# A graph attention layer and a dot-product attention layer on one core: x1 made in the head buffer in groups of four row tiles beside two held row tiles of layer 1; x1 transposes in pairs; finer pieces and VectorE sums in entry 0

## Chip, core and metric

The kernel runs on one core of a Trainium2 chip, in float32. The core has a matrix engine (TensorE, PE in the profile, with PEld for its weight loads), a vector engine (VectorE, DVE), a scalar engine (ScalarE, ACT), GpSimd (POOL) and SyncE (SP), which here only issues DMA transfers. Each engine works through its own queue in order; engines wait for one another with semaphores. The metric is the device time of one execution in microseconds. Times below come from three runs and from one further execution that the hardware profiler recorded.

## What is computed

There are B = 8 entries of N = 2048 nodes and D = 256 channels, one 0/1 adjacency matrix for all, and two layers. Layer 0 has H = 8 heads of 32 channels with an additive score; layer 1 has one head with a dot-product score. Each layer adds its input and normalizes the rows. The reference, cut to that:

```python
def layer0(x, adj, W, a_src, a_dst, beta_tilde, W_out):
    x_proj = einsum('bnd,hdf->bhnf', x, W)
    e = leaky_relu(e_src[..., :, None] + e_dst[..., None, :], 0.2)   # e_src, e_dst: x_proj times a_src, a_dst
    e = e + (softplus(beta_tilde) * log(adj + 1e-6))
    attn = softmax(where(adj > 0, e, -max), axis=-1)
    h = einsum('bhij,bhjf->bhif', attn, x_proj)
    return h.transpose(0, 2, 1, 3).reshape(B, N, D) @ W_out.T

def layer1(x, adj, W1, W2, W3):
    e = leaky_relu(einsum('bnd,bmd->bnm', x @ W1, x @ W2), 0.2)
    attention = softmax(where(adj > 0, e, -1e12), axis=-1)
    return relu(einsum('bnm,bmd->bnd', attention, x @ W3))

x = layernorm(x + layer0(x, adj, ...))       # called x1 below
x = layernorm(x + layer1(x, adj, ...))       # the output
```

## The kernel before

*Tiles.* Nodes go in NT = 16 row tiles of P = 128; channels in KC = 2 halves of 128; heads in NP = 4 pairs. PSUM has three tiles of 128 x 512 for passing results (`mm_tile`, tag "mm"), and one place each for `val`, `den` (128 x 1024) and `acc`. SBUF pools hold buffers by tag: "s" has four, "c" three, "mt", "d" and "p" two each, "pen" one, "ht" (in the pool `chunk`) three, "row" four. A buffer comes free when its last reader is done.

*Layer 0.* `Gat.project` (L225) loads x, transposes it, and multiplies it by the weights and by the score vectors; from that come v (values times exp of the destination score), re (two factors per node and head) and the rows c (a function of the source score), which for entries 1 to 7 are stored in DRAM and loaded back by `load` (L283) and `query_rows` (L289). The softmax is written so that an unnormalized weight is s = max(c, re) * mt, where mt is a row tile of the transposed adjacency raised to beta. One *unit* is one head pair and one row tile jt (`Gat.step`, L295): two DVE instructions make s for the two heads (L311, 128 x 2048 each); PE multiplies them by v into `val`, and by exp of the destination score into `den`, the denominators (both through `products`, L336). For row tiles in a list per entry, `SUMMED` (L67), the second product is left out; instead DVE keeps running sums d of s times that factor (L318; the first is a copy on ACT, L324), and at jt = 15 a product with ones adds the two sums to `den` (L329). Entry 0 has an empty list. With the last unit of a head pair, `finish` (L340) copies val and den out of PSUM on ACT, sends the denominators through DRAM to get their reciprocals in the right shape (four transfers, a reciprocal, a store, and after every second pair four loads into `rb`), and multiplies the heads by them (L363). An entry has 64 units.

*Between the layers.* `output` (L365) loads x into the buffer "h3"; for each of the 16 row tiles it multiplies the heads by W_out (y, L376), adds x (L378), normalizes (`layer_norm`, L199, with four ACT instructions on one column each, L206 to L209, and the scaling, L210) and stores x1 to DRAM through SP (L380). `turn` (L383) transposes x1, a row tile at a time, into the buffer "x1t" and multiplies it by W3 (L396), overwriting "h3".

*Layer 1.* `Dot` (L402): `queries` (L411) multiplies x1 by W1 W2^T for 512 rows; `scores` (L420) makes a row tile's scores, prelu on the way out of PSUM (L428), mask and row maximum on DVE (L431), exp on ACT (L432). One *step* (L435) is one row tile: it transposes the exponentials (L445), makes the next row tile's scores (L426), and multiplies by h3 into `acc` (L461); then it scales, adds x1 (loaded again, L466), normalizes, and stores the row tile of the output through SP (L471). A step takes a function `fill`, called at its start, after the scores and at its end (k = 0, 1, 2), which puts other work there.

*Order.* PE's instructions run in the order of the program text (`manual_schedule`, L86). A scheduler orders the other engines. So the loop at the end sets the order:

```python
    for k in range(NP * NT):
        gats[0].step()
        ...
    for b in range(1, B + 1):
        ...
        if dot is not None:
            dot.step()
        layer_0(2)
        for k, _ in enumerate(gat.output()):
            if k % 8 == 7:
                layer_0(1)
        for k, _ in enumerate(gat.turn()):
            if k % 2 == 1:
                layer_0(1)
        dot = Dot(gat)
        dot.step(lambda k: layer_0((2, 1, 1)[k]))
        for i in range(NT - 2):
            dot.step(lambda k: layer_0((0, 2 - (i % 2 == 1), 2 - (i % 14 == 13))[k]))
    dot.step()
```

Here `layer_0(n)` runs n units of entry b, and the first `dot.step()` is row tile 15 of entry b - 2. Entry 0 runs its 64 units alone, in the first head pair together with `make_mt` (L163), which makes the 16 tiles mt from the adjacency (ACT Ln and Exp, DVE, PE transposes, four ACT copies) and stores them, and throughout with 42 pieces of the other entries' projections (six an entry: four of 512 rows each, the scaling of v, the rows c) and from the second pair on with pieces of `later_weights`. After that, 12 units of entry b stand in the boundary between entry b - 1's layers, and 52 in its layer 1 steps. The last boundary and the last layer 1 have no units beside them.

Of the kernel before, what the change touches and what calls it, by code (L numbers as in the profile page):

```python
# [18 lines left out]
P = 128  # L19
# [8 lines left out]
def kernel(  # L28
# [38 lines left out]
    SUMMED = [(), (1, 3, 6, 9, 12)] + [(1, 3, 6, 8, 11, 13)] * (B - 2)  # L67
# [39 lines left out]
    def load_x(b, half):  # L107
        xr = wide.tile([P, NT // 2, D], F32, tag="p", name="xr", bufs=2)
        nc.sync.dma_start(xr, x[b].rearrange("(t p) d -> p t d", p=P)[:, ts(half, NT // 2), :])
        return xr  # L110

    first_x = [load_x(0, half) for half in range(2)]


# [18 lines left out]
    def later_weights():  # L133
# [3 lines left out]
        for w, dst in ((w_out, wot), (w1, w1t), (w2, w2t)):  # L137
            src = wide.tile([P, KC, D], F32, tag="pen", name="square", bufs=1)
            nc.sync.dma_start(src, w.rearrange("(k p) c -> p k c", p=P))
            yield  # L140
            for kc in range(KC):
                t = mm_tile("sq_t")
                for o in range(KC):
                    nc.tensor.transpose(t[:, ts(o, P)], src[:, o, ts(kc, P)], ident)
                nc.scalar.copy(dst[:, kc, :], t[:, 0:D])
# [17 lines left out]
    def make_mt(jt):  # L163
# [7 lines left out]
        nc.vector.scalar_tensor_tensor(m, a, 0.0, m, ALU.is_gt, ALU.mult)  # L171
        mt = wide_tile("mt", "mt", 2)
# [43 lines left out]
    class Gat:  # L216


        def __init__(self, b):
            self.b = b  # L220
            self.units = ((hp, jt) for hp in range(NP) for jt in range(NT))
            self.hts = []
            self.mts = []

        def project(self):  # L225
# [6 lines left out]
            xrs, xts = [], []  # L232

            def turn(g):
                if g % 2 == 0:
                    xrs.append(load_x(b, g // 2) if b > 0 else first_x[g // 2])
                xt = chunk.tile([P, KC, BK], F32, tag="ht", name="xt", bufs=3)
                for kc in range(KC):
                    t = mm_tile("tr")
                    for k in range(IG):  # L240
                        nc.tensor.transpose(t[:, ts(k, P)], xrs[-1][:, g % 2 * IG + k, ts(kc, P)], ident)
                    nc.scalar.copy(xt[:, kc, :], t)
                xts.append(xt)

            turn(0)
            for g in range(NB):
                if g + 1 < NB:
                    turn(g + 1)
                for k in range(IG):
                    it = g * IG + k  # L250
                    t = mm_tile("proj")
                    for kc in range(KC):
                        nc.tensor.matmul(t[:, 0:D + 2 * H], xts[g][:, kc, ts(k, P)], wp[:, kc, :],
                                         start=(kc == 0), stop=(kc == KC - 1))
                    nc.scalar.copy(v[:, it, :], t[:, 0:D])
                    nc.scalar.copy(both[:, it, :], t[:, D:D + 2 * H])
# [38 lines left out]
        def step(self, count=1):  # L295

            for _ in range(count):
# [6 lines left out]
                while first and len(self.mts) < min(jt + 2, NT):  # L304
                    self.mts.append(make_mt(len(self.mts)))
# [9 lines left out]
                chain = SUMMED[self.b]  # L315
# [5 lines left out]
                if jt in chain[:1]:  # L321
                    self.sums = [wide_tile("d", "d", 2) for _ in heads]
# [17 lines left out]
        def finish(self, hp):  # L340
# [3 lines left out]
            if lo == 0:  # L344
                self.hts.append(whole.tile([P, N], F32, name=f"ht{hp // 2}"))
            ht = self.hts[-1]
            for s in range(2):
                nc.scalar.copy(ht[lo:lo + HP * DH, ts(s, HALF)], self.val[ts(s, HP * DH), :])
# [14 lines left out]
            nc.vector.tensor_mul(ht, ht, rb)  # L363

        def output(self):  # L365
# [3 lines left out]
            self.h3 = h3 = whole.tile([P, NT, D], F32, tag="h3", name="h3")  # L369
            xb = x[b].rearrange("(t p) d -> p t d", p=P)  # L370
            for g in range(NB):
                nc.sync.dma_start(h3[:, ts(g, IG), :], xb[:, ts(g, IG), :])
            for it in range(NT):
                y = mm_tile("y")
                for g, ht in enumerate(self.hts):
                    nc.tensor.matmul(y[:, 0:D], ht[:, ts(it, P)], wot[:, g, :], start=(g == 0), stop=(g == 1))  # L376
                z = h3[:, it, :]
# [167 lines left out]
```

## Time and profile before

| | us |
| --- | --- |
| median of three runs | 4469.75 (4466.98 to 4470.57) |
| the profiled execution | 4467.18 |
| its span | 4465.4 |
| end of entry 0's last unit | 538.7 |
| first L416 product of entries 0 to 7 | 633.3, 1151.4, 1664.2, 2176.5, 2687.1, 3200.0, 3712.4, 4189.2 |
| from the last of these to the end | 276.2 |
| idle time of DVE before its waits for an mt transfer | 19.9 |
| wait of SP's queue for z before the stores of the output (L471) | 698.3 |

Three kinds of stretch follow one another. Entry 0's layer 0 fills the first 538.7 us. Then come, for each entry, a boundary (from the last unit of the entry's layer 0 to the first L416 product) and a layer-1 stretch; a period of the two is 510.6 to 518.1 us between the first L416 products of entries 0 to 6. The last period is shorter by the missing units, and after it comes the last layer 1.

In the rows of the profile, a name such as `s<-c,re,mt` gives output and inputs of an instruction by the program's names; L311 is line 311 of the kernel above. Where a wait is given in square brackets, it is the idle time of that engine ahead of the row and the instruction that ended it. A page's busy shares are means over all stages, so a stage has to be read by a window of its own.

### The profile page before, as it was taken

How to read it: one execution, taken by the hardware profiler on the slowest of the kernel's cores; microseconds unless marked ns; L12 is line 12 of the kernel's file. 1: busy time of each engine (PE TensorE's matmuls, PEld its weight loads, DVE VectorE, ACT ScalarE, POOL GpSimd, SP SyncE). 2: the span in 40 equal slices, each digit the busy share in tenths (PEclk: the TensorE clock that was granted, in tenths of full speed). 3: DMA queues.
4: the chain of work that ended last, by engine and by line, in shares of the span. 5: the costliest groups of instructions: out<-in, count | busy, mean ns of one | idle time of the engine just before them, and what ended most of it. 6: DMA issues, size and time to landing. Idle time of an engine off the chain costs nothing.

```text
span 4465.4 us, 60558 instructions
## 1 busy us (share of the span) xinstructions
PE 4267.6 (96%) x24988; PEld 2217.3 (50%) x24988; DVE 3631.8 (81%) x2605; ACT 1758.7 (39%) x3611; POOL 7.5 (0%) x14
## 2 busy tenths in 40 slices
PE   6899899999999999999999999999999999999899
PEld 4444344445455545555455544545454554554566
DVE  5778798888989988988899888888988888898222
ACT  5622233334333343334333343333433343333555
POOL 0000000000000000000000000000000000000000
PEclk8999999999999999999999999999999999999999
DMA  7777665666555555556555565555545565553211
GB/s 217 262 264 263 249 218 204 220 233 217 180 189 193 182 193 184 188 181 224 176 182 178 186 213 187 189 181 207 194 160 190 189 216 183 187 182 134 69 50 41
DMA packets 252773, 843.62 MB, mean 189 GB/s; under 512 B 33616, under 2 KB 152400, under 8 KB 176976
## 3 DMA queue, kind: packets, MB, share of 16 engines
q1 hardware_dynamic: 252496, 839.74, 54.0%
q8 instruction: 196, 3.21, 0.3%
q14 instruction: 81, 0.66, 0.0%
HBM read 763.76 MB, written 75.37 MB: 188 GB/s over the span
## 4 chain that ended last, share of the span: by engine, by line
PE 60%; DVE 14%; issue 8%; ACT 4%; DMA 1%; SPq 0%; DVEq 0%; ACTq 0%
PE acc L461 17%; PE e L426 15%; PE val L336 12%; DVE s L311 9%; PE den L336 8%; PE pt L445 4%; DVE d L318 3%; PE h1p L416 2%; ACT p L432 1%; PE h3p L396 1%; ACT h L210 1%; DVE p L431 1%; PE y L376 1%; DMA mt<-mt_d 0%; ACT f L206 0%
## 5 line engine op out<-in xcount | busy, mean ns | idle before, releaser
L311 DVE SCALAR_TENSOR_TENSOR s<-c,re,mt 128x2048 f32<-128x2048 f32 x1024 | 2350.6, 2343 | 209.6 <-PE den L336 159.9
L336 PE MATMUL val<-s,v 128*32 128x512 f32 x8192 | 1045.3, 607 | 78.7 <-DVE s L311 78.5
L461 PE MATMUL acc<-h,pts 128*128 128x256 f32 x4096 | 950.6, 380 | 14.9 <-ACT pts L447 14.4
L426 PE MATMUL e<-x1t,h 128*128 128x512 f32 x2048 | 904.0, 594 | 0.0
L461 PEld LDWEIGHTS acc<-h,pts 128*128 128x128 f32 x4096 | 748.2, 190 | 107.7 <-ACT pts L447 21.8
L336 PE MATMUL den<-s,re 128*32 128x512 f32 x5568 | 709.2, 598 | 0.0
L318 DVE SCALAR_TENSOR_TENSOR d<-s,re,d 128x2048 f32<-128x2048 f32 x272 | 632.4, 2343 | 0.0
L426 PEld LDWEIGHTS e<-x1t,h 128*128 128x128 f32 x2048 | 379.6, 190 | 450.1 <-issue 417.9
L336 PEld LDWEIGHTS val<-s,v 128*32 128x32 f32 x8192 | 240.9, 110 | 697.8 <-issue 526.3
L447 ACT COPY pts<-pt 128x512 f32<-128x512 f32 x512 | 296.1, 583 | 664.7 <-PE pt L445 664.4
L428 ACT ACTIVATE p<-e 128x512 f32<-128x512 f32 x512 | 302.5, 595 | 432.3 <-PE e L426 432.3
L431 DVE CUSTOM_DVE_ANT_0 p<-p,pen 128x2048 f32<-128x2048 f32 x128 | 292.7, 2287 | 205.9 <-ACT p L428 205.6
L336 PEld LDWEIGHTS den<-s,re 128*32 128x32 f32 x5568 | 194.2, 112 | 426.7 <-issue 426.6
L432 ACT ACTIVATE p<-p,neg 128x2048 f32<-128x2048 f32 x128 | 256.7, 2005 | 272.5 <-DVE neg L431 272.5
L445 PEld LDWEIGHTS pt<-ident,p 128*128 128x128 f32 x2048 | 238.0, 141 | 223.5 <-issue 167.2
L445 PE MATMUL pt<-ident,p 128*128 128x128 f32 x2048 | 318.7, 279 | 5.4 <-ACT p L432 5.4
L469 DVE TENSOR_TENSOR z<-z,x1r 128x256 f32<-128x256 f32 x128 | 54.0, 422 | 205.4 <-ACT z L468 197.0
L468 ACT ACTIVATE z<-acc,rec 128x256 f32<-128x256 f32 x128 | 60.6, 473 | 355.9 <-PE acc L461 330.3
L376 PE MATMUL y<-wot,ht 128*128 128x256 f32 x512 | 129.6, 414 | 37.4 <-DVE ht L363 36.3
L206 ACT ACTIVATE f<-mv,eps_ln 128x1 f32<-128x1 f32 x256 | 74.2, 290 | 199.0 <-DVE mv L204 198.1
L396 PE MATMUL h3p<-w3s,x1t 128*128 128x256 f32 x512 | 133.4, 386 | 12.3 <-ACT x1t L392 12.3
L376 PEld LDWEIGHTS y<-wot,ht 128*128 128x128 f32 x512 | 104.7, 208 | 68.3 <-DVE ht L363 39.2
(76 smaller groups left out, 2083.6 us busy)
## 6 DMA issues: line engine op xcount, KB each, us to landing
mt<-mt_d SPq DMA_DIRECT2D x496, 1024.0 KB, 4.8
c<-c_d SPq DMA_DIRECT2D x64, 1024.0 KB, 6.7
pen<-pen_d SPq DMA_DIRECT2D x112, 512.0 KB, 3.3
xr<-in_x_dram SPq DMA_DIRECT2D x16, 1024.0 KB, 7.1
adj_t<-in_adj_dram SPq DMA_DIRECT2D x16, 1024.0 KB, 6.8
mt_d<-mt SPq DMA_DIRECT2D x16, 1024.0 KB, 5.6
rb<-rec_d SPq DMA_DIRECT2D x64, 256.0 KB, 4.0
h<-in_x_dram SPq DMA_DIRECT2D x32, 512.0 KB, 5.9
```

Source lines behind the costliest of these rows:

```text
L311: nc.vector.scalar_tensor_tensor(sa, self.cs[a], self.re[:, 0, jt, h:h + 1], mt, ALU.max, ALU.mult)
L318: nc.vector.scalar_tensor_tensor(d, sa, e[:, jt - 1, h:h + 1], d, ALU.mult, ALU.add)
L336: nc.tensor.matmul(dst[ts(q, DH), ts(c, BK)], weights[q % 2], s[q % 2][:, ds(q // 2 * HALF + c * BK, BK)], start=start, stop=stop)
L376: nc.tensor.matmul(y[:, 0:D], ht[:, ts(it, P)], wot[:, g, :], start=(g == 0), stop=(g == 1))
L396: nc.tensor.matmul(t[:, 0:D], x1t[:, kc, ts(it - 1, P)], w3s[:, kc, :], start=(kc == 0), stop=(kc == KC - 1))
L426: nc.tensor.matmul(t, self.h1[:, kc, ts(it % IG, P)], self.x1t[:, kc, ts(c, BK)], start=(kc == 0), stop=(kc == KC - 1))
L428: nc.scalar.activation(p[:, ts(c, BK)], t, AF.Prelu, alpha=ALPHA)
L431: nc.vector.tensor_tensor_reduce(p, p, pen, -1.0, FMAX, ALU.add, ALU.min, neg)
L432: nc.scalar.activation(p, p, AF.Exp, bias=neg, scale=-1.0, accum_out=den)
L445: nc.tensor.transpose(t[:, ts(k, P)], p[:, ts(g * IG + k, P)], ident)
L447: nc.scalar.copy(pt, t)
L461: nc.tensor.matmul(acc, now[:, ts(k, P)], self.h3[:, j, :], start=(j == 0), stop=(j == NT - 1))
```

## The change

The diff has five parts.

1. *Entry 0.* `SUMMED[0]` gets six row tiles, used by head pairs 1 to 3 (in the first, `first`, the list is empty); the running sums lie in the buffers "p". Projection pieces are one row tile of 128 each (18 an entry, 126 in all), and are done four units before entry 0's end. x for them is loaded in groups of four row tiles through the buffer "pen", one ahead. `make_mt` is split: `make_m` runs one row tile earlier. The square weights are loaded in halves into "row" buffers.
2. *Head buffer.* The two buffers `ht0` and `ht1` become one, tag "heads", with a row tile's two channel halves side by side. x1 is made in place in it, where it lay in "h3" before.
3. *Output.* `output` works in groups of four row tiles: y in pairs (one 512-wide add for two row tiles), statistics for each row tile, then Ln, Exp and a product for four columns at once (`f4`), four scalings, and one store of x1 for four row tiles. x is loaded in groups of four through the "ht" buffers of `chunk`, three at first and the fourth after the first group.
4. *Turn.* Transposes and W3 products go by two row tiles, with one 512-wide ACT copy each; a unit follows every pair.
5. *Order and queues.* The last two steps of layer 1, row tiles 14 and 15 of the entry before, are held back behind the end of the entry's units; row tile 14 has two units of the next entry beside it, row tile 15 has the four groups of `output` (1, 1 and 2) and two units. The other steps carry 4, 4 and 3 units in turn. Stores of the output and of x1 are issued by ACT instead of SP.

```diff
-    SUMMED = [(), (1, 3, 6, 9, 12)] + [(1, 3, 6, 8, 11, 13)] * (B - 2)
+    SUMMED = [(1, 3, 6, 8, 11, 13), (1, 3, 6, 9, 12)] + [(1, 3, 6, 8, 11, 13)] * (B - 2)
...
         for w, dst in ((w_out, wot), (w1, w1t), (w2, w2t)):
-            src = wide.tile([P, KC, D], F32, tag="pen", name="square", bufs=1)
-            nc.sync.dma_start(src, w.rearrange("(k p) c -> p k c", p=P))
+            src = [row_tile("square") for _ in range(KC)]
+            for o in range(KC):
+                nc.sync.dma_start(src[o], w[ts(o, P), :])
...
+    def x_groups():
+        for b in range(1, B):
+            for g in range(NB):
+                xg = wide.tile([P, IG, D], F32, tag="pen", name="xg", bufs=1)
+                nc.sync.dma_start(xg, x[b].rearrange("(t p) d -> p t d", p=P)[:, ts(g, IG), :])
+                yield xg
...
-    def make_mt(jt):
+    def make_m(jt):
         a = wide.tile([P, NT, P], I32, tag="d", name="adj_t", bufs=2)
...
         nc.vector.scalar_tensor_tensor(m, a, 0.0, m, ALU.is_gt, ALU.mult)
+        return m
+
+    def make_mt(jt, m):
         mt = wide_tile("mt", "mt", 2)
...
             def turn(g):
-                if g % 2 == 0:
-                    xrs.append(load_x(b, g // 2) if b > 0 else first_x[g // 2])
+                if b == 0:
+                    xr = first_x[g // 2][:, ds(g % 2 * IG, IG), :]
+                else:
+                    xr = ahead.pop() if ahead else next(groups)
...
+                if b > 0:
+                    ahead.extend(xg for xg in [next(groups, None)] if xg is not None)
             turn(0)
-            for g in range(NB):
-                if g + 1 < NB:
+            for it in range(NT):
+                g, k = divmod(it, IG)
+                t = mm_tile("proj")
...
+                nc.scalar.copy(v[:, it, :], t[:, 0:D])
+                nc.scalar.copy(both[:, it, :], t[:, D:D + 2 * H])
+                if k == 0 and g + 1 < NB:
                     turn(g + 1)
...
                 yield
...
                 while first and len(self.mts) < min(jt + 2, NT):
-                    self.mts.append(make_mt(len(self.mts)))
+                    at = len(self.mts)
+                    while len(self.ms) < min(at + 1 + (jt > 0), NT):
+                        self.ms.append(make_m(len(self.ms)))
+                    self.mts.append(make_mt(at, self.ms[at]))
...
-                chain = SUMMED[self.b]
+                chain = () if first else SUMMED[self.b]
...
-                    self.sums = [wide_tile("d", "d", 2) for _ in heads]
+                    self.sums = [wide_tile("d", "d" if self.b else "p", 2) for _ in heads]
...
-            if lo == 0:
-                self.hts.append(whole.tile([P, N], F32, name=f"ht{hp // 2}"))
-            ht = self.hts[-1]
+            if hp == 0:
+                self.ht = whole.tile([P, NT, KC, P], F32, tag="heads", name="ht")
+            ht = self.ht[:, :, hp // 2, :]
...
         def output(self):
...
-            for g in range(NB):
-                nc.sync.dma_start(h3[:, ts(g, IG), :], xb[:, ts(g, IG), :])
-            for it in range(NT):
-                y = mm_tile("y")
-                for g, ht in enumerate(self.hts):
-                    nc.tensor.matmul(y[:, 0:D], ht[:, ts(it, P)], wot[:, g, :], start=(g == 0), stop=(g == 1))
-                z = h3[:, it, :]
-                nc.vector.tensor_add(z, y[:, 0:D], z)
-                layer_norm(z)
-                nc.sync.dma_start(x1_d[b, ts(it, P), :], z)
-                yield
+            def load(g):
+                xs.append(chunk.tile([P, IG, D], F32, tag="ht", name="xg", bufs=3))
+                nc.sync.dma_start(xs[g], xb[:, ts(g, IG), :])
+            for g in range(NB - 1):
+                load(g)
+            for g in range(NB):
+                if g == 1:
+                    load(NB - 1)
...
+                z = self.ht[:, ts(g, IG)].rearrange("p t k i -> p t (k i)")
+                for k in range(0, IG, 2):
+                    y = mm_tile("y").rearrange("p (t c) -> p t c", t=2)
+                    for i in range(2):
+                        for kc in range(KC):
+                            nc.tensor.matmul(y[:, i, :], self.ht[:, g * IG + k + i, kc, :], wot[:, kc, :],
+                                             start=(kc == 0), stop=(kc == KC - 1))
+                    nc.vector.tensor_add(z[:, k:k + 2, :], y, xs[g][:, k:k + 2, :])
+                    for i in range(k, k + 2):
+                        nc.vector.bn_stats(st[:, i, :], z[:, i, :])
+                        nc.vector.bn_aggr(mv[:, i, :], st[:, i, :])
+                f = small.tile([P, 2, IG], F32, name="f4", bufs=2)
+                nc.scalar.activation(f[:, 0, :], mv[:, :, 1], AF.Ln, bias=eps_ln)
+                nc.scalar.activation(f[:, 0, :], f[:, 0, :], AF.Exp, scale=-0.5)
+                nc.vector.scalar_tensor_tensor(f[:, 1, :], mv[:, :, 0], -1.0, f[:, 0, :], ALU.mult, ALU.mult)
+                for k in range(IG):
+                    nc.scalar.activation(z[:, k, :], z[:, k, :], AF.Identity, bias=f[:, 1, k:k + 1],
+                                         scale=f[:, 0, k:k + 1])
+                nc.scalar.dma_start(x1_d[b].rearrange("(t p) d -> p t d", p=P)[:, ts(g, IG), :], z)
+                yield
...
         def turn(self):
...
-            for it in range(NT + 1):
-                if it < NT:
+            for j in range(NT // 2 + 1):
+                if j < NT // 2:
                     t = mm_tile("tr1")
                     for kc in range(KC):
-                        nc.tensor.transpose(t[:, ts(kc, P)], h3[:, it, ts(kc, P)], ident)
-                    nc.scalar.copy(x1t[:, :, ts(it, P)], t[:, 0:D].rearrange("p (k i) -> p k i", k=KC))
+                        for i in range(2):
+                            nc.tensor.transpose(t[:, ts(kc * 2 + i, P)], self.ht[:, 2 * j + i, kc, :], ident)
+                    nc.scalar.copy(x1t[:, :, ts(j, 2 * P)], t.rearrange("p (k i) -> p k i", k=KC))
...
-            nc.sync.dma_start(out[self.b, ts(it, P), :], z)
+            nc.scalar.dma_start(out[self.b, ts(it, P), :], z)
...
-    pieces = (B - 1) * (NB + 2)
+    pieces = (B - 1) * (NT + 2)
     for k in range(NP * NT):
         gats[0].step()
-        for _ in range((k + 1) * pieces // (NP * NT) - k * pieces // (NP * NT)):
+        due = [min(i * pieces // (NP * NT - 4), pieces) for i in (k, k + 1)]
+        for _ in range(due[1] - due[0]):
             next(others)
...
-        if dot is not None:
-            dot.step()
-        layer_0(2)
-        for k, _ in enumerate(gat.output()):
-            if k % 8 == 7:
-                layer_0(1)
-        for k, _ in enumerate(gat.turn()):
-            if k % 2 == 1:
-                layer_0(1)
+        rows = gat.output()
...
+        if dot is None:
+            layer_0(2)
+            for _ in range(2):
+                output(2)
+                layer_0(1)
+        else:
+            dot.step(lambda k: layer_0((0, 0, 2)[k]))
+            dot.step(lambda k: (output((1, 1, 2)[k]), layer_0((0, 1, 1)[k])))
+        for _ in gat.turn():
+            layer_0(1)
         dot = Dot(gat)
         dot.step(lambda k: layer_0((2, 1, 1)[k]))
-        for i in range(NT - 2):
-            dot.step(lambda k: layer_0((0, 2 - (i % 2 == 1), 2 - (i % 14 == 13))[k]))
+        for i in range(NT - 3):
+            dot.step(lambda k: layer_0((0, 2 - (i % 3 == 2), 2)[k]))
+    dot.step()
     dot.step()
```

## The prediction

> **What bounds the kernel now.** I read the page's busy shares, then the busy time by stage, then the order of time where TensorE (PE) stood still.
>
> ```profile
> PE 4267.6 (96%) x24988; PEld 2217.3 (50%) x24988; DVE 3631.8 (81%) x2605; ACT 1758.7 (39%) x3611; POOL 7.5 (0%) x14
> ...
> L311 DVE SCALAR_TENSOR_TENSOR s<-c,re,mt 128x2048 f32<-128x2048 f32 x1024 | 2350.6, 2343 | 209.6 <-PE den L336 159.9
> ```
>
> PE leads, VectorE (DVE) follows. The 96% is a modelled busy share and a mean over stages, so the stages decide. Columns of the next view: stretch, its length, busy time (instructions) of PE, PEld, DVE, ACT, POOL, granted clock, DMA share, GB/s.
>
> ```profile
> 54.00:212.00 158.00, 130.39 (x910) 72.08 (x913) 122.09 (x63) 101.00 (x158) 0.36 (x1) 0.92 0.80 258
> 212.00:538.70 326.70, 295.96 (x2068) 131.84 (x2060) 253.74 (x124) 75.03 (x244) 6.03 (x6) 0.96 0.70 255
> 538.70:633.30 94.60, 79.03 (x485) 37.00 (x482) 86.08 (x82) 34.49 (x117) 0.00 (x0) 0.91 0.60 206
> 3104.90:3200.00 95.10, 85.18 (x516) 45.55 (x512) 83.23 (x84) 39.57 (x125) 0.00 (x0) 0.95 0.57 198
> 3200.00:3617.20 417.20, 415.83 (x2432) 209.69 (x2432) 367.99 (x236) 158.34 (x270) 0.00 (x0) 1.00 0.53 187
> 4130.20:4189.20 59.00, 44.60 (x213) 37.62 (x210) 17.96 (x53) 33.14 (x122) 0.00 (x0) 0.88 0.32 97
> ```
>
> The rows are: entry 0's first head pair; its other three; then, from the end of an entry's last layer-0 unit (call it T) to L416 of its layer 1, the first such boundary and one of six steady ones; a layer-1 stretch (15 steps, 52 units); the last boundary. The layer-1 stretch is PE from end to end at clock 1.00. Time can be had in the boundaries and in entry 0. In the boundary PE waits for the head product, and DVE's own queue holds it up:
>
> ```profile
> 3119.85 0.70 PE L376 MATMUL y<-wot,ht 128*128 128x256 f32 x2
> 3125.13 2.50 PE L376 MATMUL y<-wot,ht 128*128 128x256 f32 x5 [4.58 <-DVE ht L363]
> ...
> 3100.19 0.43 DVE L469 TENSOR_TENSOR z<-z,x1r 128x256 f32<-128x256 f32 x1 [4.44 <-ACT z L468]
> 3103.27 4.61 DVE L311 SCALAR_TENSOR_TENSOR s<-c,re,mt 128x2048 f32<-128x2048 f32 x2 [1.97 <-PE den L336]
> ...
> 3154.47 9.13 DVE L311 SCALAR_TENSOR_TENSOR s<-c,re,mt 128x2048 f32<-128x2048 f32 x4
> 3163.52 2.35 DVE L318 SCALAR_TENSOR_TENSOR d<-s,re,d 128x2048 f32<-128x2048 f32 x1
> ```
>
> Four s products take 9.05 us start to start, 2.26 each. From 3154 to 3200 DVE has no gap: it, not PE, ends the boundary.
>
> **Prices.** From the order of time after 3215: a row tile's first transposes 0.49, its scores 6.97 (3216.38 to 3223.35), its weighted sum 8.22 (3227.41 to 3235.63); a step without units is 15.7 us. A unit is 1.74 (val) plus 1.72 (den, unless the sums have it). A pair of s, or of running sums, is 4.52 on DVE.
>
> **Six steady boundaries.** An entry's last unit now stands in step 13, not 14, so one whole step moves behind T. The stretch before T falls by 15.7 to 401.5 us with the same 52 units. DVE's work there stays 368 less one p reduction of 2.3: 91% instead of 88%, in lumps of two sum pairs. I charge 1 us of new waits (bounds 0 and 6).
>
> Behind T I follow the order in which the built kernel queues its instructions, by hand (new lines are marked so). Step 14 takes PE to T+15.7, two units to T+21.0. In the last boundary, where DVE is idle, the head product L363 starts at T+16.7 (4146.9 against 4130.2) and takes 2.3; so the 4.58 us wait is covered. On SP the load of v, nine transfers of the denominators and three x loads stand ahead of unit 2's mt load, which has until T+28; the fourth x load waits for the first adds (T+25) with unit 3's mt load behind it, which at 4.8 us to land is in time for T+36. Then:
> - y of four row tiles ends at T+28.4. DVE takes each two tiles as one add, two statistics, two aggregates: 0.7 + 0.8 + 0.4 = 1.9. The 512-wide add isn't in the trace; between one and two of the 256-wide (0.41, L378) I take 0.7. In DVE's queue one s of unit 2 stands behind the third add and the other behind the fourth: done at T+34.6. PE waits 6.
> - unit 2, the weighted sum, y of the last four pairs of tiles, val of unit 3: PE at T+55.5. The s of units 3 and 4 and one sum pair hold DVE to T+49.2, the last two groups' normalization to T+58. The last aggregate is queued behind an s; ACT has that group's Ln ahead of the first x1t copy, for which new L439 waits: PE stands about 5, to T+61.
> - unit 4 ends at T+66.4 and frees the s buffers of unit 6. Six units and two sum pairs on DVE, 36.2, end at T+102.6; the last val at T+104.4.
>
> So this part grows from 95.1 to 104.4 while 15.7 leaves the stretch before: -6.4, with the new waits -5.4, times six = -32. If all three waits vanish it stays 95.1: -15.7 each. If they grow by half it is 112: +1. I take what the replay gives, since the order is fixed and its durations stand in rows.
>
> A rule speaks against groups of four. The rows: L206 to L209 take 0.29, 0.20, 0.19 and 0.29 us for one column each, on ACT at 39%. The Trainium skill (Perfetto Trace Analysis, Optimizing Scalar/DVE Operations) has grouping pay on a saturated engine, and smaller pieces where an unsaturated one makes others wait. By it the saved columns buy nothing and the wait before T+61 is their price; with finer pieces unit 6 would start 4.2 earlier and the six would give -58.
>
> **Last boundary** (59.0). No s work: y from T+19.2, the weighted sum between, last y at T+42.3; the last group's Ln frees the copies at T+46; eight pairs of 0.43 + 1.74 make T+63.5. With the step moved: -15.7 + 4.5 = -11 (bounds -16 and -3). **First boundary** (94.6). 12 units as before. PE waits 9.93 before its first val, for c rows behind the last est; those now come four units earlier, but v can't be loaded until its last use, 7.9 us (v<-v_d, median): -2 (bounds -6 and +4).
>
> **Entry 0.** First head pair, 158 us: m is made one tile earlier, so Ln and Exp (2.0 each) run under two s products. A unit needs on DVE 2 x 2.26 + 2.20 + 1.13 = 7.9 (83.44 to 85.64, 87.90 to 89.03), on ACT 4.0 + 2.4 for four mt copies + 1.8 for two pieces of projection = 8.2; DMA is already at 0.80. I take 8.9, and 5.4 for one scaling of v (L260 to L270): 148, so -10 (bounds -27, by DVE alone, and 0). Other three pairs, 326.7 us: 15 den products leave PE (-25.8), 30 sums come to DVE (30 x 2.26 = 67.9); six 2.0 us copies go to ACT, busy 23% there. DVE then needs 321.6 and PE 270, the latter spread evenly by pieces of one row tile: DVE is the bound, -5. This is the loosest guess: if only half of the 73 us that DVE idles there now goes, +31; if the 0.08 by which its records overlap comes off each, -15.
>
> **Queues, copies, weights.** Outputs and x1 leave SP for ACT. SP waited 698.3 us on z for the outputs (its waits), but DVE only 19.9 for mt: bounds -20 and 0, and I take 0, as the stretch where outputs run has no PE gap to give. SP issues an output in 0.34; ACT's issue is not shown, 0 to 0.58 (four x loads in 2.31), 20 an entry, covered by PSUM's three score tiles; uncovered it is 8 x 20 x 0.34 = 54. Copies of 512 for two of 256 (583 ns against 372 twice) lie behind DVE: 0. The weights in halves lie under entry 0's DVE: 0.
>
> The page DMA: Bandwidth & Descriptors, Issuing engines are not separate DMA queues, grants a second issuing engine only its issue time: by it 0.34 x 128 = 44 us of SP and nothing on the path. The page PSUM — Partial Sum Buffer, Engine vs sequencer instructions, calls ScalarE's queue strictly first in, first out; no row here shows what a transfer in it costs.
>
> **Sum.** -32 - 11 - 2 - 10 - 5 = -60. The profiled execution took 4467.18 us (span 4465.4); the median of the runs, 4469.75, is 2.6 above. 4467.2 - 60 + 2.6 = 4410.
>
> **Rivals.**
> - *DVE gives it back.* Steady boundaries end at T+109.8, net 0, and entry 0 gains nothing: -11 - 2 = -13, 4457. For it: DVE is busy 88% of the boundary already. Against: DVE idles 4.44 + 1.97 + 2.25 + 4.69 + 1.98 = 15.3 us before its rows from 3100 to 3118, which the moved step fills.
> - *The waits I charge vanish.* 6 x (-15.7 + 1) - 16 - 2 - 10 - 5 = -121, 4349. For it: L311 at 3091.10 shows an entry's first s done long before T. Against: only four s buffers.
> - *ACT's queue becomes the gate (slower).* A moved transfer may have to wait on ACT for an earlier one that holds its completion semaphore; Prelu and copies stand behind, and PE runs only two score tiles ahead (2 x 1.74 = 3.5 us). At mt's 4.8 to land plus 0.34 PE loses 1.6 an output: 128 x 1.6 = +205, 4615. It decides from 3.5 + 60/128 = 4.0 us held. For it: nearly all moved transfers carry such a wait in the new order. Against: the earlier transfer lies about a step (28 us) back.
>
> **Numbers.** Forecast 0.54, first rival 0.18, second 0.16, slower 0.12. The likeliest gives 4410 (alone 4385 to 4435). The range reaches over the first rival and into the second, and leaves out the slower one and the second's far half: 4360 to 4462. 0.2% (9 us) is what a measurement here can tell from no change; of the first rival 0.06 falls within it: faster 0.82, same 0.06, slower 0.12.
>
> **What would show it.** From one entry's first queries product (L416, new L459) to the next, 507 us instead of 512.4; no PE gap before the first y, but 6 before unit 2 and 5 before the first L439; a layer-1 stretch near 402 without PE gaps; DVE near 95% busy from entry 0's second head pair on, and its T near 523 instead of 538.7. I am wrong if ACT waits at DMA rows between Prelus, if entry 0 passes 550, or if a boundary stays under 97.

## The result, and the profile after

The changed kernel takes 4463.76 us (median of four runs, 4461.57 to 4465.11) against 4469.22 beside it: a ratio of 0.9988, 95% interval 0.9971 to 1.0005. That is 5.5 us, and not told from no change; 4410 was forecast. The profiled execution spans 4462.5 us against 4465.4, 2.9 shorter. Cut into the prediction's stages (T is the end of an entry's last layer-0 unit):

| stage, us | before | forecast | after |
| --- | --- | --- | --- |
| T of entry 0 | 538.7 | 523.7 | 559.5 |
| first boundary | 94.6 | 92.6 | 95.3 |
| steady boundary (from 3105) | 95.1 | 104.4 | 105.6 |
| layer-1 stretch behind it | 417.9 | 402.5 | 403.3 |
| period, first L416 (L459) product to the next | 512.4 | 507 | 508.6 |
| last boundary | 59.0 | 63.5 | 63.1 |
| last layer 1 | 276.2 | 276.2 | 276.2 |

The boundary and the stretch that were replayed came out within 1.2 us. (The prediction's row for the stretch before, 417.2, ends 0.7 us ahead of its last product; measured to that product it is 417.9.) Entry 0 did not: 20.8 us longer where 15 shorter were forecast. That is 35.8 of the 57 us between the forecast change (-60) and that of the profiled executions (-2.9). The six steady boundaries have another 17.3, the first boundary 2.7 and the last 1.1. The page's lines for the two engines, and DVE's two large groups:

```profile
PE 4254.7 (95%) x24748; PEld 2217.8 (50%) x24748; DVE 3688.7 (83%) x2603; ACT 1682.0 (38%) x3041; POOL 13.4 (0%) x14
...
L330 DVE SCALAR_TENSOR_TENSOR s<-c,re,mt 128x2048 f32<-128x2048 f32 x1024 | 2354.2, 2342 | 178.8 <-PE den L355 117.7
...
L337 DVE SCALAR_TENSOR_TENSOR d<-s,re,d 128x2048 f32<-128x2048 f32 x302 | 701.7, 2344 | 0.0
```

There are 240 fewer matmuls and 30 more running sums, as the prediction counted them; the sums went from 632.4 to 701.7 us. The busy time by stage, with the columns of the prediction's view:

```profile
56.00:212.00 156.00, 135.10 (x920) 72.28 (x921) 122.83 (x63) 101.65 (x162) 0.36 (x1) 0.89 0.80 253
212.00:559.50 347.50, 293.12 (x1813) 130.19 (x1811) 326.24 (x157) 86.07 (x247) 11.95 (x6) 0.91 0.69 247
559.50:654.80 95.30, 76.75 (x483) 39.91 (x480) 79.78 (x76) 24.24 (x43) 0.00 (x0) 0.89 0.58 194
3105.00:3210.60 105.60, 96.72 (x579) 55.04 (x576) 85.13 (x85) 35.95 (x69) 0.00 (x0) 0.97 0.59 200
3210.60:3613.90 403.30, 401.71 (x2373) 199.38 (x2370) 365.13 (x231) 150.77 (x255) 0.00 (x0) 1.00 0.54 189
4123.20:4186.30 63.10, 58.09 (x274) 46.95 (x274) 20.79 (x55) 31.14 (x66) 0.00 (x0) 0.97 0.33 101
```

The second row is entry 0's head pairs 1 to 3. DVE is busy 326.2 us there, near the 321.6 of the forecast, but in 347.5 us: 94%, not all of it. That is the "near 95% busy" that the prediction gave as a sign; at 95%, 321.6 us of work take 338.5, so that the sign and the -5 did not go together. PE is busy 293.1 us with 1813 matmuls where it took 296.0 for 2068 before; the granted clock is 0.91 against 0.96, so the 15 products that left bought no PE time.

In order of time, the steady boundary shows the waits that the prediction named (PE first, then DVE; h3p is x1 times W3):

```profile
3125.92 3.72 PE L408 MATMUL y<-wot,ht 128*128 128x256 f32 x16
...
3135.05 1.04 PE L355 MATMUL val<-s,v 128*32 128x512 f32 x2 [1.52 <-DVE s L330]
3138.70 2.78 PE L355 MATMUL val<-s,v 128*32 128x512 f32 x11 [2.60 <-DVE s L330]
...
3165.86 1.99 PE L439 MATMUL h3p<-w3s,x1t 128*128 128x256 f32 x8 [2.70 <-ACT x1t L434]
```

```profile
3132.05 0.69 DVE L410 TENSOR_TENSOR ht<-y,xg 128x512 f32<-128x512 f32 x1
3132.66 2.34 DVE L330 SCALAR_TENSOR_TENSOR s<-c,re,mt 128x2048 f32<-128x2048 f32 x1
...
3135.66 0.66 DVE L410 TENSOR_TENSOR ht<-y,xg 128x512 f32<-128x512 f32 x1
...
3136.33 2.32 DVE L330 SCALAR_TENSOR_TENSOR s<-c,re,mt 128x2048 f32<-128x2048 f32 x1
```

PE has no gap before the first y. It waits 1.52 + 2.60 before unit 2 (6 forecast), whose two s stand behind the third and the fourth add, as said, and 2.70 before the first h3p (5 forecast).

### The profile page after: what moved, and what is told of

The parts are those of the page before. It is cut to its first block, busy times and chain, and to the rows that moved or that the text cites. A ratio compares the mean times of both kernels' runs of the same rounds, so it can differ in the third digit from the quotient of the medians.

```text
span 4462.5 us, 59194 instructions
## 1 busy us (share of the span) xinstructions
PE 4254.7 (95%) x24748; PEld 2217.8 (50%) x24748; DVE 3688.7 (83%) x2603; ACT 1682.0 (38%) x3041; POOL 13.4 (0%) x14
## 4 chain that ended last, share of the span: by engine, by line
PE 60%; DVE 14%; issue 7%; DMA 3%; ACT 2%; SPq 0%; ACTq 0%; DVEq 0%
PE acc L504 16%; PE e L469 15%; PE val L355 12%; DVE s L330 9%; PE den L355 8%; PE pt L488 4%; DVE d L337 4%; DMA mt<-mt_d 2%; PE y L408 2%; PE h1p L459 2%; PE h3p L439 1%; DVE p L474 0%; ACT p L475 0%; DMA rc<-dn 0%; DVE ht L410 0%
## 5 line engine op out<-in xcount | busy, mean ns | idle before, releaser
L337 DVE SCALAR_TENSOR_TENSOR d<-s,re,d 128x2048 f32<-128x2048 f32 x302 | 701.7, 2344 | 0.0
L355 PE MATMUL den<-s,re 128*32 128x512 f32 x5280 | 677.6, 602 | 3.2 <-ACT dn L370 3.2
L267 PE MATMUL proj<-wp,xt 128*128 128x272 f32 x512 | 142.0, 419 | 11.8 <-DVE wp L125 8.0
L439 PE MATMUL h3p<-w3s,x1t 128*128 128x256 f32 x512 | 124.0, 386 | 17.1 <-ACT x1t L434 16.2
L343 ACT ACTIVATE d<-s,re 128x2048 f32<-128x2048 f32 x62 | 124.3, 2008 | 35.4 <-DVE ht L383 24.6
L408 PE MATMUL y<-wot,ht 128*128 128x256 f32 x512 | 119.4, 390 | 15.8 <-DVE ht L383 15.8
```

The costliest lines, as they stand in the source:

```text
L337: nc.vector.scalar_tensor_tensor(d, sa, e[:, jt - 1, h:h + 1], d, ALU.mult, ALU.add)
L355: nc.tensor.matmul(dst[ts(q, DH), ts(c, BK)], weights[q % 2], s[q % 2][:, ds(q // 2 * HALF + c * BK, BK)], start=start, stop=stop)
L408: nc.tensor.matmul(y[:, i, :], self.ht[:, g * IG + k + i, kc, :], wot[:, kc, :], start=(kc == 0), stop=(kc == KC - 1))
L439: nc.tensor.matmul(t[:, ts(i, D)], x1t[:, kc, ts(2 * (j - 1) + i, P)], w3s[:, kc, :], start=(kc == 0), stop=(kc == KC - 1))
```

## What held entry 0: four experiments

In the first head pair of the changed kernel, PE stands still at the start of each projected entry (m is a row tile of the adjacency raised to beta, before the transposes mtp that make mt of it):

```profile
159.61 0.38 SPq L167 DMA_DIRECT2D xg<-in_x_dram  x1
...
164.06 1.75 PE L256 MATMUL tr<-ident,xg 128*128 128x128 f32 x8 [3.02 <-DMA xg<-in_x_dram]
...
170.44 1.23 DVE L178 TENSOR_SCALAR m<-adj_t 128x2048 f32<-128x2048 int32 x1 [10.16 <-PE mtp L190]
```

The first piece of an entry transposes two x groups, and the one buffer "pen" lets the second load start (159.61) only when the first is read. PE waits 3.02, and behind it in its queue stand the mt transposes that DVE waits 10.16 for. Seven such waits come to 24.3 us on PE; six waits for est (the transpose that gives the rows c), which now follows the scaling of v within the same unit, to 18.6. Two theories: DVE is the bound through the sums (A), or PE's queue is (B).

**No sums in entry 0.**

```diff
-    SUMMED = [(1, 3, 6, 8, 11, 13), (1, 3, 6, 9, 12)] + ...
+    SUMMED = [(), (1, 3, 6, 9, 12)] + ...
```

> Entry 0 of the changed kernel ends its last unit at 559.5 us (T), not at the 523 forecast and 20.8 later than before. Theory A (the sums): DVE, busy 326 of 347.5 us in head pairs 1 to 3, sets that stretch, and every wait of it is lost; without the 30 sums it needs 257 and PE gets 15 denominator products, 25.8 us, back: PE busy 293 + 26 - 7 = 312, plus the waits of before's kind, so the stretch falls to about 330 and T to about 542. Theory B (PE's queue): PE is held by waits in its own queue, for the second x group of an entry (24.3 us in 7 waits) and for the est transpose (18.6 in 6); these stay and PE has more to do: T stays at 559 or grows to 575.

Measured: 4442.04 us, ratio to before 0.9944 (0.9929 to 0.9959); T 535.2. That goes with theory A, and is 7 us better than it said. T is 24.3 us earlier, which is more than the 20.8 that entry 0 lost.

**The second x group two row tiles later.**

```diff
-                if k == 0 and g + 1 < NB:
+                if k == 2 and g + 1 < NB:
```

> The second x group of an entry is transposed two row tiles later, so that its load (5 us to land) can be hidden; every product and sum stays. Theory A: in head pairs 1 to 3 DVE's 326 us stay the bound and T falls only by the two long DVE waits for PE in the first head pair (10.7 and 10.2 us, each followed by an x wait of 3): by 10 to 20 us, the stretch behind 212 by under 5. Theory B: the seven x waits go in both parts: T falls by 24 us or more, half of it behind 212. If both are wrong, T stays within 3 us of 559.5.

Measured: 4449.57 us, 0.9963 (0.9950 to 0.9976); T 545.0. From the first val product of head pair 1 to T, the three kernels read:

```profile
214.40:559.50 345.10, 291.68 (x1806) 129.30 (x1806) 324.02 (x156) 84.48 (x242) 11.95 (x6) 0.91 0.68 246
```

```profile
211.50:535.20 323.70, 294.12 (x2046) 129.17 (x2046) 255.79 (x125) 71.92 (x236) 10.00 (x6) 0.95 0.70 253
```

```profile
204.60:545.00 340.40, 293.00 (x1806) 125.83 (x1806) 323.69 (x156) 84.14 (x242) 11.95 (x6) 0.93 0.69 248
```

The first is the changed kernel, the second the one without sums, the third the one with the later group. PE's busy time hardly differs, though the second has 240 matmuls more. The sums cost 21.4 us of head pairs 1 to 3. The later group gives 9.8 us in the first head pair (its end goes from 214.4 to 204.6) and 4.7 behind it, where DVE covers it: A on both counts.

**The est transpose one more unit later.** Two empty pieces between the scaling of v and est:

```diff
             yield
+            yield
+            yield
             t = mm_tile("est")
...
-    pieces = (B - 1) * (NT + 2)
+    pieces = (B - 1) * (NT + 4)
```

> Two empty pieces between the scaling of v and the est transpose of each entry, so that about one more unit lies between them. Theory A: T stays within 4 us of 559.5, since DVE idles only 0.3 us at each of these places. Theory B: the est waits (18.6 us on PE) go and T falls by 10 to 18.

Measured: 4466.11 us, 0.9999 (0.9990 to 1.0009); T 561.6. Nothing, as A has it.

**Entry 0 as before the change.** Projection, `make_mt`, weights and x loads of the kernel before, no sums; all that follows as changed.

```diff
-    pieces = (B - 1) * (NT + 2)
+    pieces = (B - 1) * (NB + 2)
...
-        due = [min(i * pieces // (NP * NT - 4), pieces) for i in (k, k + 1)]
-        for _ in range(due[1] - due[0]):
+        for _ in range((k + 1) * pieces // (NP * NT) - k * pieces // (NP * NT)):
```

> Entry 0 as before the change (coarse pieces, m with mt, no sums, loads through p), everything behind it as changed. If the two halves of the change do not touch each other: T back at 538.7 within 3 us, the boundaries and layer-1 stretches as in the changed kernel (105.5 and 403), so the time is the changed kernel's less 20.8: 4443. If entry 0's new form also paid for something behind it (c rows of entry 1 four units earlier), the first boundary grows from 95.3 by up to 10 and the time is up to 4453.

Measured: 4445.67 us, 0.9952 (0.9938 to 0.9967); T 538.6, boundaries 105.6 to 106.3, first boundary 96.8. The two halves of the change hardly touch each other (the first boundary is 1.5 longer): the boundaries give 21.6 us (4467.27 before, beside it, less 4445.67), and the new entry 0 takes back 18.1 (4463.76 - 4445.67).

## Balancing entry 0: four more

**Both: no sums and the later group.**

> Both edits that helped: the second x group two row tiles later, and no sums in entry 0. Theory A (with the sums DVE is the bound of head pairs 1 to 3 and covers PE's x waits, without them PE is the bound and every x wait counts): the first head pair falls by 14 us as in the run with the later group alone, and behind it PE loses its x waits (20.8 us over entry 0 in the run without sums, some 14 of them here): T at 535.2 - 14 - 10 = 511 (505 to 517), time 4418. If the x waits behind 212 are covered in this form too, T is 521 and the time 4428.

Measured: 4418.18 us, 0.9893 (0.9877 to 0.9910); T 511.8, as expected.

```profile
204.00:511.80 307.80, 289.35 (x2046) 126.86 (x2046) 255.64 (x126) 71.59 (x236) 10.00 (x6) 0.97 0.73 267
```

With the sums the later group was worth 14.5 us of T, without them 23.4 (535.2 to 511.8): with DVE off the bound, PE's waits count. PE is now busy 94% of head pairs 1 to 3, at clock 0.97. Against entry 0 of before, T is 26.9 us earlier: the rest of the new entry 0 does pay, without the sums that came with it.

**Later group with three summed row tiles** (`SUMMED[0] = (1, 6, 11)`).

> Later x group with three row tiles a head pair in the sums in place of six (two denominator products less on PE net, two pairs of running sums on DVE): DVE needs 257 + 12 x 2.26 = 284 us in head pairs 1 to 3, PE some 283. If one engine's need is the bound, this lies at or below the run without sums. If the two engines hinder one another where their needs are near (four s buffers, uneven pieces), it lies above it by 5 to 10 us.

Measured: 4433.98 us, 0.9927 (0.9912 to 0.9942); T 523.0, which is 11.2 above no sums (5 to 10 expected from hindrance) and 22.0 below six. Both needs (DVE 284, PE 283 by the expectation) lie 34 us below the 318.4 that head pairs 1 to 3 took, so neither alone explains it. That each engine's lumps make the other wait fits, but no run isolates it.

**m not made ahead**, on no sums and the later group:

```diff
-                    while len(self.ms) < min(at + 1 + (jt > 0), NT):
+                    while len(self.ms) < min(at + 1, NT):
```

> No sums and the later x group, but m made no tile ahead, as before the change. By the prediction Ln and Exp (2.0 us each) then lie on the path of each row tile's mt: the first head pair, 141.2 us with m ahead, grows by 10 or more (to 151 to 158). Rival: DMA (busy 0.86 of that stretch) or DVE (121.7 of 140 us) sets the first head pair, and m ahead is worth nothing: 141 within 3.

Measured: 4417.7 us, 0.9883 (0.9868 to 0.9897); first head pair 141.8 against 141.2. The step of the prediction that gave the 10 us to m ahead is wrong: it is worth nothing here.

**est later, on no sums and the later group.**

> No sums and the later x group, and the est transpose of each entry one more unit behind the scaling of v. With the sums this did nothing (T 561.6 against 559.5). If PE is the bound of head pairs 1 to 3 now, its est waits (9.7 us in 6, three to six of them behind 212) count: T falls from 511.8 by 5 to 10. If they are covered, T stays within 3.

Measured: 4425.52 us, 0.9901 (0.9884 to 0.9917); T 517.0, that is 5.2 later, where 5 to 10 earlier or no change was expected. The first head pair ends 4.1 earlier (200.3), the rest takes 9.3 more. The empty pieces also change how pieces fall on units; why that costs is open.

## The boundary: four more

**Row tile 15 alone held back.**

```diff
-            dot.step(lambda k: layer_0((0, 0, 2)[k]))
+            layer_0(2)
             dot.step(lambda k: (output((1, 1, 2)[k]), layer_0((0, 1, 1)[k])))
...
-        for i in range(NT - 3):
-            dot.step(lambda k: layer_0((0, 2 - (i % 3 == 2), 2)[k]))
-    dot.step()
+        for i in range(NT - 2):
+            dot.step(lambda k: layer_0((0, 2 - (i % 2 == 1), 2 - (i % 14 == 13))[k]))
     dot.step()
```

> The changed kernel with row tile 15 alone held back, as before the change, and the units of the layer-1 steps as before (two units, then row tile 15 with the four output groups and two units). By the prediction the moved row tile 14 covers PE's wait for the head product and DVE's idle time: without it the first y waits for the product at about T + 15, the stretch is 418 again, and the boundary falls by less than the 15.7: period 513 to 518 in place of 508.6, time up by 25 to 60. Rival: pairs and groups alone make the gain, the held row tile nothing: period at 508.6 or below.

Measured: 4534.75 us, 1.0150 (1.0134 to 1.0165); period 518.8: 71.0 us above the changed kernel, more than the 25 to 60 expected. PE's three longest waits behind T in this kernel:

```profile
3164.55 3.64 PE L355 MATMUL val<-s,v 128*32 128x512 f32 x16 [4.99 <-DMA v<-v_d]
3177.61 6.08 PE L408 MATMUL y<-wot,ht 128*128 128x256 f32 x14 [4.57 <-DVE ht L383]
3214.14 3.59 PE L439 MATMUL h3p<-w3s,x1t 128*128 128x256 f32 x8 [4.72 <-ACT x1t L434]
```

The moved row tile covers the head product, as the prediction had it, and also the load of v, which it had priced for the first boundary alone. It is worth 10.2 us a period. The rest of the new boundary without it is slower than the old one: 518.8 against 512.4.

**Normalization columns two at a time.**

```diff
-                f = small.tile([P, 2, IG], F32, name="f4", bufs=2)
-                nc.scalar.activation(f[:, 0, :], mv[:, :, 1], AF.Ln, bias=eps_ln)
+                    f = small.tile([P, 2, 2], F32, name="f2", bufs=4)
+                    nc.scalar.activation(f[:, 0, :], mv[:, k:k + 2, 1], AF.Ln, bias=eps_ln)
...
```

> The changed kernel with normalization columns two at a time in place of four; loads and stores as they are. By the prediction the group of four is what makes PE wait before the first h3p (2.7 us here, 5 forecast), so unit 6 starts up to 4.2 earlier: period 508.6 down to 504.4 to 506, time down by 16 to 29. Rival: the last statistics are queued behind an s product on DVE in either form, the wait stays, and the added ACT instructions cost nothing: period within 0.5 of 508.6.

Measured: 4471.60 us (ten runs, 4465.02 to 4481.57), 1.0009 (1.0000 to 1.0019): 7.8 us above the changed kernel, not 16 to 29 below. The interval touches the changed kernel's (0.9971 to 1.0005), so a loss is likely and not certain; the gain did not come. ACT's order in the profiled execution:

```profile
3178.34 1.09 ACT L419 ACTIVATE ht<-ht,f 128x256 f32<-128x256 f32 x2 [1.07 <-DVE f L417]
...
3179.52 0.56 ACT L434 COPY x1t<-tr 128x512 f32<-128x512 f32 x1
```

The copy that PE's h3p waits for now stands behind a scaling (L419) that waits for a product f on DVE, itself behind an s; PE waits 3.79 there, not 2.70. The prediction weighed the Trainium skill here (Perfetto Trace Analysis, Optimizing Scalar/DVE Operations: smaller pieces where an unsaturated engine makes others wait) and worked out 26 us more of gain by it (58 in place of 32). In this place the measurement goes against it: the trace shows the copy's place in ACT's queue deciding PE's wait, and the smaller pieces moved it back.

**Stores issued by SP again.**

```diff
-                nc.scalar.dma_start(x1_d[b]...
+                nc.sync.dma_start(x1_d[b]...
...
-            nc.scalar.dma_start(out[self.b, ts(it, P), :], z)
+            nc.sync.dma_start(out[self.b, ts(it, P), :], z)
```

> The changed kernel with the stores of the output and of x1 issued by SP again. By the prediction the queue is worth nothing: period within 1 us of 508.6, time within 5 us of the changed kernel's. Rival: SP's waits for z (698 us before) come back ahead of the mt loads behind them, DVE waits for mt (20 us before) grow in the boundary where the held row tiles' outputs lie: period up by 1.5 to 5, time up by 10 to 35. If ACT's queue were the gate of the third rival, the time would fall by 20 or more; the one wait of 3.5 us on an output transfer that the changed kernel's trace shows speaks against it.

Measured: 4488.37 us, 1.0044 (1.0029 to 1.0059): 24.6 above the changed kernel, as the rival said. The layer-1 stretch is 409.4 instead of 403.3. One of its waits, in order of time (SPq is SP's queue):

```profile
3396.63 2.48 SPq L381 DMA_DIRECT2D rb<-rec_d  x3
3405.08 0.36 SPq L514 DMA_DIRECT2D out_dram<-z  x1
...
3405.96 0.92 SPq L197 DMA_DIRECT2D mt<-mt_d  x2
...
3412.18 2.35 DVE L330 SCALAR_TENSOR_TENSOR s<-c,re,mt 128x2048 f32<-128x2048 f32 x1 [6.37 <-DMA mt<-mt_d]
...
3419.90 3.64 PE L355 MATMUL val<-s,v 128*32 128x512 f32 x14 [4.28 <-DVE s L330]
```

SP is free at 3399.1, stands until 3405.08 for z, and issues the two mt loads only then; DVE waits 6.37 and PE 4.28. In the old schedule this cover was enough (19.9 us of such waits in all); with 4, 4 and 3 units a step it isn't. The move to ACT, priced at 0, is part of what the shorter stretch needs.

**The third unit of the next entry ("fresh" in the code) ahead of the first y**, on no sums and the later group:

```diff
-            dot.step(lambda k: layer_0((0, 0, 2)[k]))
-            dot.step(lambda k: (output((1, 1, 2)[k]), layer_0((0, 1, 1)[k])))
+            dot.step(lambda k: layer_0((0, 0, 3)[k]))
+            dot.step(lambda k: (output((1, 1, 2)[k]), layer_0((0, 0, 1)[k])))
```

> No sums in entry 0, the later x group, and the third fresh unit moved from behind the second output group to the end of row tile 14, so ahead of the first y. By the prediction PE's wait for unit 2 (4.1 us here, 6 forecast) comes from DVE's order, adds of the first output groups ahead of its two s products; in the new order they stand directly behind the head product, start when unit 0 frees its buffers (T + 19) and are done at about T + 23.7, so that PE waits 1 to 2 in place of 4.1: period 508.6 down to 505 to 507, time 4418 down to 4395 to 4408. Rival: DVE ends the boundary anyway, with as many s products and sums behind T as before: period within 0.6 of 508.6.

Measured: 4387.42 us, 0.9812 (0.9796 to 0.9829): 1.9% below before, the best of all. In four of the five boundaries behind entry 1's, the boundary takes 99.3 and the period is 502.2 to 502.7, better than the 505 to 507 expected. The fifth, from 3041.3, takes 101.0; its waits:

```profile
3062.96 1.04 PE L355 MATMUL val<-s,v 128*32 128x512 f32 x2 [0.74 <-DVE s L330]
3065.22 2.58 PE L355 MATMUL val<-s,v 128*32 128x512 f32 x11 [1.22 <-DVE s L330]
3097.49 1.99 PE L439 MATMUL h3p<-w3s,x1t 128*128 128x256 f32 x8 [1.38 <-ACT x1t L434]
```

The waits are the same in the other four: 1.96 us before unit 2 in place of 4.12, and 1.38 before h3p in place of 2.70. That is 3.5 of the 6.3 us between 105.6 and 99.3; most of the rest is the clock (below).

## Why the prediction was wrong, point by point

- **Other three pairs of entry 0, "DVE is the bound, -5".** This step failed. The needs were right (DVE 321.6 forecast, 326.2 busy), the reading of them was not: a stretch does not shrink to the need of its busiest engine. It took 347.5. The -5 compared a stretch where PE led, with 31 us to spare, with one where DVE would have had none. PE did not get its 25.8 us back: its busy time stayed (296.0 to 293.1), at a clock of 0.91 in place of 0.96. From the first val product of pair 1 to T these pairs went from 320.4 us to 345.1. Taking the sums out gives 21 to 33 us of it (345.1 to 323.7, and 340.4 to 307.4 with the later group, from 204.4). Why the sums cost that much while both engines' needs lie below the stretch stays open. The prediction called this its loosest guess and its upper bound, +31, holds the +20.8.
- **First head pair, -10.** It ended 3.9 earlier by the first val of pair 1 (218.3 to 214.4). Most units took 5.6 to 9.2 us, at or under the 8.9; two of 21.7 and 23.4 (from 58.4 and from 146.9) took most of the gain, at the double transposes that the working per unit left out (12.1 and 19.2 with the later group). Making m ahead, on which the -10 was built, gave nothing where it was tried.
- **Six steady boundaries, -32.** Five periods sum to -17.6 where -27 was forecast: the waits were shorter than forecast (6.8 against 11), but the slow clock after the first two (2.7 us, below) was not in the replay: the two nearly cancel, and unit 4 ended at T+66.4 as forecast. The boundary is 1.2 longer at its end: DVE had made its last s at T+102.8 (102.6 forecast), but PE, with unit 10 and an h3p still ahead in its queue, began the last unit 1.0 later. And the row of before that was taken, 95.1, is the longest of the six (92.7 to 95.1). The term's bounds, 95.1 and 112, lie some 2 us above what waits of 6 and 5 make of 104.4 (93.4 without them, 109.9 half longer). The first of the six, beside entry 0's layer 1, went the wrong way: 518.1 to 521.0. Its stretch fell by 9.7 only (425.3 to 415.6) and its boundary rose from 92.8 to 105.5. PE is busy 410.2 of those 415.6 us, with 47 more products than in the other stretches, as entry 1 sums five row tiles in place of six. The period stays at 518 to 523 in all runs but the one with one held row tile (525.2); what would shorten it was not tried.
- **Last boundary, -11.** Right: the last period fell by 9.9 (476.8 to 466.9).
- **First boundary, -2.** +0.7 here, within its bounds (-6 to +4). PE's wait of 9.93 before the first val fell to 3.88 (for v), but before the first y it now waits 12.22 for the head product (at 583.3), which the term left out. In the other runs this boundary takes 92.9 to 96.8 where T is 538 or later and 96.3 to 100.5 where it is earlier, so that some of what entry 0 gains is given back there.
- **Queues, 0.** As a term of the sum it did no harm: the stretch that has the outputs came out at 403.3 against 402.5. As the worth of the move it was wrong: back on SP the stores cost 24.6 us in the new order.
- **The rivals.** The slower one fell: ACT waits once, 3.5 us, for an output transfer in the whole changed kernel. The first, "DVE gives it back", named the total best (4457 against 4463.76), partly by luck: it named the right place for entry 0 and the wrong one for the boundaries, which gained.

## What to carry to other kernels

Moving work from the leading engine to the second one did not pay in any amount that was tried here (no, three and six row tiles in the sums: T 511.8, 523.0 and 545.0 us with the later group), although neither engine's need filled the stretch. Look at what each engine waits for, and not at the larger need alone. When a change makes pieces finer, replay its first and last piece too: here two pieces in one slot took back 23.4 of the 26.9 us that the new entry 0 gives without the sums. And the place of an instruction in an in-order queue (a store ahead of loads, a scaling ahead of a copy) decided more here than its cost.

## What the runs showed of the hardware

PE's clock can fall after quite short waits. In the changed kernel's boundary, by windows of 5 us with the granted clock third from the end, and PE's rows behind the waits there and at the end of the same boundary:

```profile
3135.00:3140.00 5.00, 2.34 (x10) 0.53 (x14) 5.00 (x11) 0.00 (x0) 0.00 (x0) 0.73 1.04 379
3140.00:3145.00 5.00, 5.00 (x27) 1.05 (x20) 5.00 (x5) 0.50 (x2) 0.00 (x0) 0.59 0.91 354
```

```profile
3138.70 2.78 PE L355 MATMUL val<-s,v 128*32 128x512 f32 x11 [2.60 <-DVE s L330]
...
3141.28 3.72 PE L355 MATMUL den<-s,re 128*32 128x512 f32 x15
...
3203.29 1.49 PE L355 MATMUL val<-s,v 128*32 128x512 f32 x11 [1.22 <-DVE s L330]
...
3204.62 2.30 PE L355 MATMUL den<-s,re 128*32 128x512 f32 x15
```

After waits of 1.52 and 2.60 us the rest of a unit's products takes 6.30 us (3138.70 to 3145.00); after waits of 0.84 and 1.22 at the end of the boundary, with the clock at 1.00, the same products take 3.63 (3203.29 to 3206.92). So 4.1 us of waiting cost 2.7 more. The Trainium skill (TensorE: Matmul & The Clock Gate, Part 1: The HAM clock gate) has the clock halve after an idle window of about 3.4 us and return after as long a busy time. The trace agrees roughly on the half and on the return; here two waits, neither of which is 3.4 long, were enough.

The length of the waits does not settle it. In the kernel with the third unit ahead of the first y, waits of 0.74 and 1.22 us stand in all five boundaries behind entry 1's. In one of them the clock fell and the rest of the unit took 5.33 us (3065.22 to 3070.55), in the other four it stayed at 1.00 and the rest took 3.63. Two of them, whole:

```profile
2036.90:2136.20 99.30, 93.91 (x580) 54.71 (x576) 84.36 (x85) 35.96 (x69) 0.00 (x0) 1.00 0.60 212
3041.30:3142.30 101.00, 95.61 (x577) 54.98 (x577) 84.27 (x85) 35.97 (x69) 0.00 (x0) 0.98 0.60 209
```

Here, then, a short PE wait costs its length, and sometimes 1.7 to 2.7 us of slow products behind it; what decides between the two was not tried.
